# Copying a second block of each cross-partition exchange with GpSimd: a fused cross-attention layer on one Trainium2 core

## Chip, cores and metric

The kernel runs on one core of a Trainium2 chip, all in float32. The metric is the time of one execution on the device in microseconds (us). A change is compared by the median of several runs.

## What is computed

A transformer layer with cross-attention, for 4 batches of 512 rows and 512 features, 16 heads of 32, and an MLP of width 2048:

```python
x = layer_norm(hidden_states, ln1_w, ln1_b)
q = (x @ q_w + q_b).reshape(B, LQ, H, HD).transpose(0, 2, 1, 3)
k = (encoder_hidden_states @ k_w + k_b).reshape(B, LK, H, HD).transpose(0, 2, 1, 3)
v = (encoder_hidden_states @ v_w + v_b).reshape(B, LK, H, HD).transpose(0, 2, 1, 3)
scores = jnp.einsum('bhqd,bhkd->bhqk', q, k) * scale
scores = jnp.where(mask, scores, mask_value)
attn = jax.nn.softmax(scores, axis=-1)
out = jnp.einsum('bhqk,bhkd->bhqd', attn, v)
out = out.transpose(0, 2, 1, 3).reshape(B, LQ, D)
hidden = out @ cproj_w + cproj_b + hidden_states
y = layer_norm(hidden, ln2_w, ln2_b)
y = jax.nn.gelu(y @ fc_w + fc_b, approximate=True)
return hidden + y @ proj_w + proj_b
```

## The kernel before

**Units of attention.** The attention is cut into 16 units w: four batches by four groups of four heads (a group fills the 128 partitions with 4 x 32 features). In the text, 5:1 is unit 5, second half of its 512 query rows. For each quarter of the query rows, `scores` (L510) multiplies q and k on TensorE into four score banks, one a head. `exps` masks a bank and takes its extreme on VectorE (L518), then ScalarE takes exponentials and their sums (L521).

**The exchange.** The probabilities lie with queries on partitions, and the product with v needs keys there. TensorE isn't used for that transposition. VectorE transposes blocks of 32 x 32, each within its group of 32 partitions (`turn`, L529, L536, and L539 for the reciprocal sums) into a buffer tb with four column blocks j. Then block j of partition group i must come to group j, as column block i of a second buffer pT: 16 blocks of 32 partitions x 1088 values for each half of a unit. The four with i = j stay in their group and GpSimd copies them (`stay`, L546). Of the twelve that cross between groups, eleven are transfers from SBUF to SBUF in SyncE's queue (`exchange`, issued by `load`, L327) and one, from group 0 to group 1, is a fifth GpSimd copy (L549). `attend` (L572) multiplies all of pT by v, so it needs all sixteen blocks; L578 scales the product by the reciprocal sums. tb, pT, the 16 units and their two halves make 32 exchanges. tb and pT are both in the tile `swap`.

**Around it.** GpSimd's queue also has bias sums (L330), the weight sums of the MLP's first matrix product (`w_sums`, tile `wsum`, L330 and L333; both products of the MLP are computed with sums of blocks that save multiplications), the layer norm's small power (`ln_rs`, L349 to L357), the sums that apply the first layer norm to a transposed x in batches 1 to 3 (`apply_stats`, L410 and L333), and transfers that it issues itself: stores of the MLP's hidden values (`gelu`, L673, from one of three staging buffers st), of the attention's result (L449) and loads of the mask (L454). ScalarE applies the layer norm's weights after `apply_stats` (`apply_weights`, L421) and copies products into staging buffers (`joins`, L650). `cproj` (L443) is the output projection, `ln_norm` (L362) and `ln_turn` (L369) are the second layer norm and its transposition by TensorE, `fc` and `project` (L625) the MLP.

**The order.** A table of tokens, ORDER, sets the order of all work: each token calls the generator of a piece of work, and each call runs it to its next `yield`. `d:w:half` is `stay`, `e:w:half` is `exchange`, `a` is `attend`, `u` is `scores`. Each engine runs its instructions in the order in which the tokens recorded them. In each exchange `stay` has three steps (two copies, two copies, the fifth), so three `d` tokens, of which other work may stand in between.

Of the kernel before, what the change touches and what calls it, by code (L numbers as in the profile page):

```python
# [86 lines left out]
u:4:2 r:4:0 r:4:1 a:3:0 x:4:2 x:4:2 k:7 r:4:1 a:3:0 x:4:2 r:4:1 r:4:1 x:4:2 c:0:1 d:3:1 v:4 d:3:1 d:3:1
# [21 lines left out]
u:7:3 na:2 g:0:1 j:0:4 wa:2 wa:2 g:0:4 r:7:1 j:0:4 q:8 q:8 g:0:4 d:6:1 d:6:1 d:7:0 d:7:0 d:7:0 e:6:1 lf:0:6 lf:0:6  # L109
  fs:0:6 g:0:4 f:0:3 lh:1 lh:1 e:7:0 e:7:0 e:7:0 x:7:3 x:7:3 r:7:2 x:7:3 x:7:3 a:6:1  # L110
# [4 lines left out]
u:8:3 d:7:1 d:7:1 v:8 j:0:3 f:0:3 f:0:5 k:11 x:8:3 x:8:3 r:8:2 r:8:2 j:0:3 e:8:0 wq:11 lf:1:0 e:8:0 le:3 le:3 lh:1  # L115
  e:8:0 a:7:1 j:0:3 r:8:3 x:8:3 x:8:3 g:0:3 r:8:3 r:8:3
u:9:0 d:8:0 fs:0:5 fs:0:5 cb:1 d:8:0 d:8:0 fs:0:5 g:0:2 v:10 g:0:2 c:1:1 x:9:0 x:9:0 x:9:0 a:7:1 x:9:0 j:0:5 k:11
  c:1:0 r:8:3 c:1:0
u:9:1 x:9:1 x:9:1 r:9:0 f:0:5 f:0:5 j:0:5 fs:0:5 d:8:1 fs:0:6 fs:0:6 d:8:1 d:8:1 cb:1 s2:1 wk:13 e:8:1 wv:12 lx:3
  e:8:1 lx:3 lf:0:7 lf:1:0 wq:12 e:8:1 wv:13 lf:1:1 f:0:7 f:0:5 c:1:3 j:0:5 r:9:1 x:9:1 x:9:1 j:0:5 f:0:5  # L120
u:9:2 g:0:3 j:0:5 r:9:1 r:9:0 r:9:1 s2:1 c:1:3 g:0:5 x:9:2 x:9:2 a:8:0 q:11 x:9:2 a:8:0 r:9:1 x:9:2
u:9:3 r:9:2 j:0:5 x:9:3 q:11 x:9:3 c:1:2 a:8:1 e:9:0 d:9:0 fs:0:7 v:9 c:1:3 fs:0:7 g:0:3 fs:0:7 d:9:0 d:9:0 v:11
# [4 lines left out]
  x:10:1 j:0:7 a:9:0 r2:1 c:1:2 c:1:0 fs:1:0 fs:1:1 fs:1:1 fs:1:1 d:9:1 d:9:1 d:9:1 fs:1:0 fs:1:0 fs:1:0 x:10:1 x:10:1  # L127
# [3 lines left out]
u:10:3 t2:1:3 t2:1:1 t2:1:0 s1:3 t2:1:2 r:10:2 t2:1:2 x:10:3 x:10:3 x:10:3 t2:1:0 v:13 r1:3 d:10:0 d:10:0 d:10:0 g:0:7  # L131
  t2:1:1 a:9:1 ts:3 ts:3 r:10:3 x:10:3
# [14 lines left out]
u:12:3 f:1:4 fs:1:4 fs:1:4 d:11:1 d:11:1 fs:1:3 g:1:2 f:1:4 j:1:3 lf:1:6 wq:15 e:11:1 r:12:1 x:12:3 j:1:4 x:12:3  # L147
  r:12:2 r:12:1 f:1:3 f:1:4 j:1:4 j:1:3 x:12:3 x:12:3
u:13:0 lh:2 fs:1:6 d:12:0 d:12:0 d:12:0 c:2:1 r:12:2 r:12:3 x:13:0 x:13:0 j:1:4 x:13:0 x:13:0 r:12:3 f:1:4 j:1:4
u:13:1 r:12:3 j:1:4 a:11:1 r:12:3 x:13:1 e:12:0 e:12:0 lf:1:7 lp:0 e:12:0 a:12:0 c:2:1 r:13:0 j:1:3 x:13:1 x:13:1  # L150
  x:13:1 a:11:1 d:12:1 d:12:1 d:12:1 fs:1:6 cb:2 fs:1:5 fs:1:5 c:2:0 a:12:0 r:13:0
# [3 lines left out]
  x:13:3 r:13:2 x:13:3 s2:2 c:2:3 fs:1:6 g:1:4 r2:2 d:13:0 d:13:0 d:13:0 a:12:1 a:12:1  # L155
# [84 lines left out]
def xattn_block(ctx: ExitStack, tc: tile.TileContext, x, x_t, encT, mask, q_w, k_w, v_w, c_w, w_fc, p_w, vecs, rows, out):  # L240
    nc = tc.nc
# [48 lines left out]
    pt = ptt.rearrange("p (s c n) -> p s c n", s=3, c=NP)  # L290
# [35 lines left out]
    def load(o, i):  # L326
        nc.sync.dma_start(out=o, in_=i)  # L327
# [215 lines left out]
    def stay(w, half):  # L543
        tb, pT = tb_of[half], pT_of[half]
        for i in range(NI):
            nc.gpsimd.tensor_copy(pT[ts(i, HD), i], tb[ts(i, HD), i])  # L546
            if i % 2:
                yield
        nc.gpsimd.tensor_copy(pT[ts(1, HD), 0], tb[ts(0, HD), 1])  # L549
# [303 lines left out]
    for _ in range(WARM):  # L853
# [70 lines left out]
```

## Time and profile before

| | |
|---|---|
| median of 3 runs | 759.24 us (757.78 to 760.06) |
| the profiled execution | 760.55 us |
| its span, first to last instruction | 758.7 us |
| busy: TensorE (PE) | 750.4 us |
| busy: VectorE (DVE) | 597.8 us |
| busy: ScalarE (ACT) | 403.1 us |
| busy: GpSimd (POOL) | 406.3 us in 433 instructions |

The profile was taken of one execution. A group's row has line, engine, operation, output <- input, count, then busy time in us and mean duration in ns, then the idle time of its engine just before, with what ended it. A row of a timeline has start and duration in us, the same names, and in brackets the engine's idle time before it. Rows of waits read "who <- for whom: us in total, times, longest". SPq is the queue of SyncE, which issues transfers. The profile's line numbers are those of the kernel before.

### The profile page before, as it was taken

What the parts mean: (1) busy time and instruction counts of PE and PEld (TensorE: products, weight loads), DVE (VectorE), ACT (ScalarE), POOL (GpSimd) and SP (SyncE); (2) the same over time, 40 slices, a digit from 0 to 9 for tenths busy, and PEclk for the clock granted to TensorE, in tenths of its full rate; (3) what the DMA queues carried; (4) which work ended last, traced back from release to release, by engine and by line L of the source; (5) the groups of instructions that cost most, each with busy time, mean ns of one, the idle gap of its engine ahead of it and who ended that gap; (6) DMA issues with size and microseconds to landing.
All of it is one profiled execution on the core that took longest, in us unless ns stands there. A gap on an engine that the chain in (4) does not pass through costs nothing.

```text
span 758.7 us, 14111 instructions
## 1 busy us (share of the span) xinstructions
PE 750.4 (99%) x4925; PEld 532.9 (70%) x4925; DVE 597.8 (79%) x1209; ACT 403.1 (53%) x951; POOL 406.3 (54%) x433
## 2 busy tenths in 40 slices
PE   9999999999999999999999999999999999999998
PEld 6464555367665456665655677766888999999997
DVE  3798999999868888876788986644789799786982
ACT  2566766466777776778867686761343221211110
POOL 1166975864996767666858767954401022140232
PEclk9999999999999999999999999999999999999999
DMA  7688877867886797775877598779545647888575
GB/s 267 211 237 231 231 194 225 224 178 215 201 227 201 217 245 241 192 227 141 230 223 202 181 273 240 222 254 317 162 139 175 245 138 160 229 168 261 100 181 111
DMA packets 70598, 157.73 MB, mean 208 GB/s; under 512 B 11448, under 2 KB 24144, under 8 KB 68864
## 3 DMA queue, kind: packets, MB, share of 16 engines
q1 hardware_dynamic: 55328, 126.98, 57.7%
q0 software_dynamic: 15056, 29.84, 15.7%
q8 instruction: 39, 0.64, 0.3%
q14 instruction: 31, 0.25, 0.1%
q10 hardware_dynamic: 144, 0.02, 0.0%
HBM read 73.95 MB, written 25.18 MB: 131 GB/s over the span
## 4 chain that ended last, share of the span: by engine, by line
PE 90%; DMA 4%; SPq 2%; DVE 2%; POOL 1%; issue 1%; ACT 0%; POOLq 0%; ACTq 0%
PE acc L625 34%; PE sc L625 11%; PE sc L510 8%; PE acc L487 8%; PE acc L443 7%; PE acc L497 7%; PE acc L572 7%; PE acc L475 7%; SPq L327 2%; DMA gd<-st 2%; PE acc L369 1%; DMA swap<-swap 1%; DMA ptt<-v_w_dram 1%; DMA pbt<-fc_w_dram 1%; PE acc L854 0%
## 5 line engine op out<-in xcount | busy, mean ns | idle before, releaser
L521 ACT ACTIVATE ptt<-ptt,mn 128x512 f32<-128x512 f32 x256 | 182.9, 716 | 77.8 <-DVE mn L518 77.3
L518 DVE CUSTOM_DVE_ANT_0 ptt<-sc,mix 128x512 f32<-128x512 f32 x256 | 164.5, 679 | 29.4 <-PE sc L510 28.0
L546 POOL COPY swap<-swap 32x1088 f32<-32x1088 f32 x128 | 139.6, 1090 | 56.8 <-DVE swap L539 36.0
L529 DVE STREAM_TRANSPOSE swap<-ptt 128x1024 f32<-128x1024 f32 x64 | 78.8, 1231 | 9.3 <-DMA pbt<-fc_w_dram 4.3
L536 DVE STREAM_TRANSPOSE swap<-ptt 128x1024 f32<-128x1024 f32 x64 | 78.2, 1224 | 1.8 <-ACT ptt L521 1.8
L510 PE MATMUL sc<-pbt 32*128 32x512 f32 x512 | 73.9, 640 | 0.8 <-ACT pbt L489 0.8
L673 POOL DMA_DIRECT2D gd<-st x32 | 24.6, 772 | 91.5 <-ACT st L671 82.7
L650 ACT COPY st<-acc 128x256 f32<-128x256 f32 x96 | 34.3, 367 | 70.8 <-PE acc L625 66.2
L497 PEld LDWEIGHTS acc<-ptt,ext 128*128 128x128 f32 x512 | 58.6, 192 | 9.3 <-issue 2.9
L625 PE MATMUL acc<-ys,wsum 128*128 128x256 f32 x256 | 64.3, 383 | 0.7 <-ACT st L650 0.7
L572 PE MATMUL acc<-swap,mix 128*32 128x256 f32 x1024 | 61.5, 382 | 0.1
L497 PE MATMUL acc<-ptt,ext 128*128 128x128 f32 x512 | 60.9, 277 | 0.3 <-DMA ptt<-v_w_dram 0.3
L625 PE MATMUL acc<-yT,pbt 128*128 128x256 f32 x240 | 59.0, 386 | 1.4 <-DVE mix L578 1.4
L650 ACT COPY xn<-acc 128x128 f32<-128x128 f32 x75 | 18.9, 270 | 77.4 <-PE acc L625 72.6
L475 PE MATMUL acc<-ext,ptt 128*128 128x512 f32 x128 | 58.5, 599 | 0.0
L487 PE MATMUL acc<-ext,ptt 128*128 128x512 f32 x128 | 58.4, 600 | 0.0
L625 PEld LDWEIGHTS acc<-yT,pbt 128*128 128x128 f32 x240 | 44.0, 190 | 20.2 <-issue 6.9
L443 PE MATMUL acc<-mix 128*128 128x512 f32 x128 | 58.0, 599 | 0.0
L625 PEld LDWEIGHTS acc<-ys,wsum 128*128 128x128 f32 x256 | 47.5, 190 | 13.3 <-issue 2.2
L572 PEld LDWEIGHTS acc<-swap,mix 128*32 128x32 f32 x1024 | 30.4, 109 | 31.4 <-issue 9.0
L330 DVE TENSOR_TENSOR st<-acc,st 128x512 f32<-128x512 f32 (+1 forms) x48 | 26.1, 544 | 32.6 <-ACT st L650 22.7
L810 POOL DMA_DIRECT2D swap<-xn x18 | 22.3, 1506 | 52.2 <-DVE xn L330 16.7
(144 smaller groups left out, 1458.2 us busy)
## 6 DMA issues: line engine op xcount, KB each, us to landing
swap<-swap SPq DMA_DIRECT2D x352, 136.0 KB, 3.3
gd<-st POOLq DMA_DIRECT2D x32, 512.0 KB, 4.5
swap<-gd SPq DMA_DIRECT2D x12, 1024.0 KB, 5.1
pbt<-fc_w_dram SPq DMA_DIRECT2D x40, 256.0 KB, 3.9
xn<-x_dram SPq DMA_DIRECT2D x32, 256.0 KB, 4.8
ext<-fc_w_dram SPq DMA_DIRECT2D x24, 256.0 KB, 2.8
swap<-xn POOLq DMA_DIRECT2D x18, 256.0 KB, 4.9
ptt<-k_w_dram SPq DMA_DIRECT2D x16, 256.0 KB, 4.2
```

Of the source, the lines that this page charges most:

```text
L443: nc.tensor.matmul(acc, oT[:, g, ts(t, P)], wc[:, g, :], start=(g == 0), stop=(g == NG - 1))
L475: nc.tensor.matmul(acc, S["wk", w][:, d, :], eT[:, d, :], start=(d == 0), stop=(d == ND - 1))
L487: nc.tensor.matmul(acc, S["wq", w][:, d, :], xT[:, d, :], start=(d == 0), stop=(d == ND - 1))
L497: nc.tensor.matmul(acc[:, ts(t, P)], eT[:, d, ts(t, P)], S["wv", w][:, d, :], start=(d == 0), stop=(d == ND - 1),)
L510: nc.tensor.matmul(sc[h], S["qT", w][r, ts(qt, P)], S["kT", w][r, :], start=True, stop=True)
L518: nc.vector.tensor_tensor_reduce(out=s, in0=sc[h], in1=mb, scale=1.0, scalar=FMAX, op0=ALU.add, op1=ALU.min, accum_out=mn)
L521: nc.scalar.activation(s, s, AF.Exp, bias=mn, scale=-1.0, accum_out=S["sums", w][:, qt, h : h + 1])
L529: nc.vector.transpose(*two_heads[0])
L536: nc.vector.transpose(*two_heads[1])
L546: nc.gpsimd.tensor_copy(pT[ts(i, HD), i], tb[ts(i, HD), i])
L572: nc.tensor.matmul(av[ts(h, HD), : 2 * P].rearrange(shape, **kw), v[:, t, ts(h, HD)], p[t][h], start=(t == 0), stop=(t == NT - 1),)
L625: nc.tensor.matmul(o, x[:, k], y[:, k], start=(k == 0 and not more), stop=(k == n - 1), skip_group_check=more)
```

## The change

The block from group 2 to group 3 (i = 2, j = 3) is copied by GpSimd as well, as a sixth copy in a fourth step of `stay`; `exchange` leaves it out, so it issues ten transfers. It was the first transfer of each exchange.

```diff
@@ -548,13 +550,15 @@
         nc.gpsimd.tensor_copy(pT[ts(1, HD), 0], tb[ts(0, HD), 1])
         yield
+        nc.gpsimd.tensor_copy(pT[ts(3, HD), 2], tb[ts(2, HD), 3])
+        yield
 
     def exchange(w, half):
         tb, pT = tb_of[half], pT_of[half]
         for d in range(1, NI):
             for i in (0, 2, 1, 3):
                 j = (i + d) % NI
-                if (i, j) == (0, 1):
+                if (i, j) in ((0, 1), (2, 3)):
                     continue
                 load(pT[ts(j, HD), i], tb[ts(i, HD), j])
             yield
```

In ORDER each exchange gets a fourth `d` token, straight behind the third; the other tokens and their sequence are as they were. One line of it:

```diff
-u:1:2 r:1:1 q:2 s1:1 x:1:2 x:1:2 x:1:2 x:1:2 k:3 d:0:1 d:0:1 d:0:1 v:0 fs:0:0 r:1:2 r:1:1 q:3
+u:1:2 r:1:1 q:2 s1:1 x:1:2 x:1:2 x:1:2 x:1:2 k:3 d:0:1 d:0:1 d:0:1 d:0:1 v:0 fs:0:0 r:1:2 r:1:1 q:3
```

On TensorE, VectorE and ScalarE the instructions and their order stay the same. The changed file has four more lines, so line 546 is 548 there, 549 is 551, and the added copy is 553.

GpSimd's queue around the copies of 4:0 and 4:1 and the second layer norm's rs of batch 0, before (xn_86 and the like are rows of x, ve_0 and rs_0 the layer norm's numbers):

```order
L330 TENSOR_TENSOR xn_86<-xn_86,row 128x512
L546 COPY swap<-swap 32x1088 x2
L549 COPY swap<-swap 32x1088
L330 TENSOR_TENSOR wsum<-pbt 128x256
L333 TENSOR_TENSOR wsum<-pbt,wsum 128x256
L454 DMA m_73<-mask_dram 128x512
L330 TENSOR_TENSOR mix<-mix,row 128x512
L449 DMA xa_91<-xn_84 128x512
L546 COPY swap<-swap 32x1088 x4
L549 COPY swap<-swap 32x1088
L349 TENSOR_SCALAR ve_0_1324<-mv_0_1187 128x4
L357 TENSOR_TENSOR rs_0_1326<-ve_0_1324,nhalf 128x4
```

and with the change:

```order
L548 COPY swap<-swap 32x1088 x2
L551 COPY swap<-swap 32x1088
L553 COPY swap<-swap 32x1088
L332 TENSOR_TENSOR wsum<-pbt 128x256
L335 TENSOR_TENSOR wsum<-pbt,wsum 128x256
L456 DMA m_73<-mask_dram 128x512
L332 TENSOR_TENSOR mix<-mix,row 128x512
L451 DMA xa_91<-xn_84 128x512
L548 COPY swap<-swap 32x1088 x4
L551 COPY swap<-swap 32x1088
L553 COPY swap<-swap 32x1088
L351 TENSOR_SCALAR ve_0_1324<-mv_0_1187 128x4
```

Two copies more now stand ahead of ve_0 and rs_0.

GpSimd's queue from the copies of 6:0 to the store of the MLP's first hidden values (gd <- st), before:

```order
L546 COPY swap<-swap 32x1088 x2
L549 COPY swap<-swap 32x1088
L330 TENSOR_TENSOR wsum<-pbt 128x256
L333 TENSOR_TENSOR pbt<-pbt 128x256
L333 TENSOR_TENSOR wsum<-wsum,pbt 128x256
L410 TENSOR_TENSOR ext<-ext,xn_84 128x512
L333 TENSOR_TENSOR ext<-ext,xn_82 128x512
L673 DMA gd_95<-st_88 512x1x256
```

and with the change:

```order
L548 COPY swap<-swap 32x1088 x2
L551 COPY swap<-swap 32x1088
L553 COPY swap<-swap 32x1088
L332 TENSOR_TENSOR wsum<-pbt 128x256
L335 TENSOR_TENSOR pbt<-pbt 128x256
L335 TENSOR_TENSOR wsum<-wsum,pbt 128x256
L412 TENSOR_TENSOR ext<-ext,xn_84 128x512
L335 TENSOR_TENSOR ext<-ext,xn_82 128x512
L677 DMA gd_95<-st_88 512x1x256
```

The store stands behind one copy more.

SyncE's queue around the exchange of 1:0, whose transfers are split by the load of the layer norm's numbers (xn_86 <- sd), before:

```order
L327 DMA ext<-x_t_dram 128x512 x2
L327 DMA ext<-encT_dram 128x512 x3
L327 DMA swap<-swap 32x1088 x7
L327 DMA xn_86<-sd_100 128x512
L327 DMA swap<-swap 32x1088 x4
```

and with the change:

```order
L329 DMA ext<-x_t_dram 128x512 x2
L329 DMA ext<-encT_dram 128x512 x3
L329 DMA swap<-swap 32x1088 x6
L329 DMA xn_86<-sd_100 128x512
L329 DMA swap<-swap 32x1088 x4
```

What follows the first transfer of an exchange moves forward by one place.

More of the change, by code (lines that the diff above doesn't have):

```diff
@@ L114 @@
 u:8:2 q:9 r:8:0 r:8:1 r:8:1 x:8:2 j:0:3 r:8:1 q:9 x:8:2 q:10 x:8:2 x:8:2
[L115 to L120, printed above, removed]
+u:8:3 d:7:1 d:7:1 d:7:1 v:8 j:0:3 f:0:3 f:0:5 k:11 x:8:3 x:8:3 r:8:2 r:8:2 j:0:3 e:8:0 wq:11 lf:1:0 e:8:0 le:3 le:3
+  lh:1 e:8:0 a:7:1 j:0:3 r:8:3 x:8:3 x:8:3 g:0:3 r:8:3 r:8:3
+u:9:0 d:8:0 fs:0:5 fs:0:5 cb:1 d:8:0 d:8:0 d:8:0 fs:0:5 g:0:2 v:10 g:0:2 c:1:1 x:9:0 x:9:0 x:9:0 a:7:1 x:9:0 j:0:5
+  k:11 c:1:0 r:8:3 c:1:0
+u:9:1 x:9:1 x:9:1 r:9:0 f:0:5 f:0:5 j:0:5 fs:0:5 d:8:1 fs:0:6 fs:0:6 d:8:1 d:8:1 d:8:1 cb:1 s2:1 wk:13 e:8:1 wv:12
+  lx:3 e:8:1 lx:3 lf:0:7 lf:1:0 wq:12 e:8:1 wv:13 lf:1:1 f:0:7 f:0:5 c:1:3 j:0:5 r:9:1 x:9:1 x:9:1 j:0:5 f:0:5
 u:9:2 g:0:3 j:0:5 r:9:1 r:9:0 r:9:1 s2:1 c:1:3 g:0:5 x:9:2 x:9:2 a:8:0 q:11 x:9:2 a:8:0 r:9:1 x:9:2
-u:9:3 r:9:2 j:0:5 x:9:3 q:11 x:9:3 c:1:2 a:8:1 e:9:0 d:9:0 fs:0:7 v:9 c:1:3 fs:0:7 g:0:3 fs:0:7 d:9:0 d:9:0 v:11
+u:9:3 r:9:2 j:0:5 x:9:3 q:11 x:9:3 c:1:2 a:8:1 e:9:0 d:9:0 fs:0:7 v:9 c:1:3 fs:0:7 g:0:3 fs:0:7 d:9:0 d:9:0 d:9:0 v:11
   fs:0:6 fs:0:7 j:0:7 x:9:3 g:0:5 x:9:3 c:1:2 r:9:2 a:8:1
@@ L146 @@
   x:12:2 r:12:1 q:14 j:1:4
[L147 to L149 removed]
+u:12:3 f:1:4 fs:1:4 fs:1:4 d:11:1 d:11:1 d:11:1 fs:1:3 g:1:2 f:1:4 j:1:3 lf:1:6 wq:15 e:11:1 r:12:1 x:12:3 j:1:4
+  x:12:3 r:12:2 r:12:1 f:1:3 f:1:4 j:1:4 j:1:3 x:12:3 x:12:3
+u:13:0 lh:2 fs:1:6 d:12:0 d:12:0 d:12:0 d:12:0 c:2:1 r:12:2 r:12:3 x:13:0 x:13:0 j:1:4 x:13:0 x:13:0 r:12:3 f:1:4
+  j:1:4
 u:13:1 r:12:3 j:1:4 a:11:1 r:12:3 x:13:1 e:12:0 e:12:0 lf:1:7 lp:0 e:12:0 a:12:0 c:2:1 r:13:0 j:1:3 x:13:1 x:13:1
[L151 removed]
+  x:13:1 a:11:1 d:12:1 d:12:1 d:12:1 d:12:1 fs:1:6 cb:2 fs:1:5 fs:1:5 c:2:0 a:12:0 r:13:0
 u:13:2 r:13:1 x:13:2 g:1:3 f:1:6 c:2:3 r:13:1 g:1:3 c:2:0 x:13:2 x:13:2 g:1:4 g:1:4 r:13:1 x:13:2 c:2:2 lf:2:0 lf:2:0
@@ new lines @@
+  fs:2:4 v:15 g:2:3 x:15:2 a:14:0 f:2:4 j:2:4 f:2:4 f:2:4 j:2:4 d:14:1 d:14:1 d:14:1 d:15:0 e:15:0 e:15:0 e:15:0 f:2:5
+  j:2:2 x:15:2 f:2:4 x:15:2 j:2:4 j:2:5 x:15:2
+u:15:3 f:2:5 d:15:0 d:15:0 d:15:0 f:2:5 x:15:3 x:15:3 r:15:2 j:2:4 f:2:4 j:2:4 j:2:4 a:14:1 a:14:1 r:15:3 g:2:2 g:2:4
+  j:2:5 g:2:4 a:15:0 f:2:5 j:2:5 x:15:3 g:2:2 a:15:0 c:3:0 c:3:0 x:15:3 r:15:2 c:3:1 fs:2:6 fs:2:6 g:2:4 f:2:7 j:2:7
+  r:15:3 s2:3 j:2:5 c:3:1 r:15:3 lf:2:7 fs:2:6 f:2:5 j:2:5 j:2:5 r:15:3 g:2:2 fs:2:7 fs:2:7 fs:2:7 cb:3 la:0:1 lp:4
+  lp:3 lf:3:0 lp:3 lp:5 lf:3:1 lp:7 fs:2:6 d:15:1 c:3:1 fs:2:7 c:3:0 f:2:7 f:2:7 f:2:6 j:2:7 f:2:6 f:2:7 j:2:6 g:2:5
+  j:2:7 f:2:6 j:2:6 lf:3:1 e:15:1 e:15:1 e:15:1 lf:3:0 j:2:7 f:2:7 j:2:7 f:2:6 P:0:1 d:15:1 d:15:1 d:15:1 fs:3:1
+  fs:3:1 fs:3:0 fs:3:0 fs:3:0 fs:3:1 j:2:6 ps:2 j:2:6 ps:4 f:2:6 j:2:6 j:2:6 ps:0 a:15:1 s2:3 la:0:4 lp:7 lh:3 j:2:7
+  cb:3 ps:2 a:15:1 c:3:2 c:3:2 c:3:3 s2:3 c:3:3 s2:3 ps:0 r2:3 fs:3:0 c:3:2 la:0:2 lp:6 P:0:1 hd:0 hd:0 la:0:7 P:0:2
+  pj:0:1 g:2:6 g:2:7 g:2:7 g:2:6 g:2:5 P:0:2 pj:0:2 c:3:3 n2:3 n2:3 g:2:6 g:2:7 fs:3:1 J:0:1 g:2:5 n2:3 n2:3 t2:3:2
+  t2:3:0 t2:3:1 t2:3:0 t2:3:3 t2:3:3 t2:3:2 t2:3:1 y:3 y:3 y:3 ps:2 f:3:0 f:3:1 f:3:1 j:3:1 j:3:0 f:3:1 j:3:1 f:3:0
+  f:3:1 j:3:1 f:3:0 gs:0:5 y:3 gs:0:6 ps:4 gs:0:5 j:3:1 pt:5 pt:6 f:3:1 j:3:0 f:3:0 lf:3:3 f:3:3 j:3:0 j:3:3 j:3:1
+  g:3:1 ps:6 j:3:1 j:3:0 ps:0 pt:3 f:3:0 lr lf:3:3 lf:3:2 fs:3:3 fs:3:3 f:3:3 j:3:0 g:3:1 g:3:0 lf:3:2 fs:3:3 f:3:3
+  j:3:3 ps:2 pt:7 j:3:0 fs:3:3 gs:0:7 fs:3:2 fs:3:2 fs:3:2 fs:3:2 ps:0 f:3:2 g:3:1 f:3:3 f:3:2 j:3:2 j:3:3 g:3:0 f:3:2
+  j:3:2 j:3:3 f:3:3 f:3:2 j:3:3 g:3:3 j:3:2 lf:3:5 g:3:0 ps:6 pt:6 pt:6 xs:0:4 lf:3:4 lf:3:5 j:3:3 j:3:2 ps:4 f:3:5
+  f:3:2 lf:3:4 j:3:2 j:3:2 fs:3:5 pt:5 fs:3:5 gs:0:6 fs:3:5 xs:0:4 ps:4 fs:3:4 fs:3:4 fs:3:5 fs:3:4 fs:3:4 xs:0:4 ps:6
```

77 lines of the change are left out of this document (31 added, 46 removed).

## The prediction

> **What bounds the kernel now.** I read the busy shares first, then what TensorE waits for, and then, place by place, the timelines of the engines that feed it.
>
> ```profile
> PE 750.4 (99%) x4925; PEld 532.9 (70%) x4925; DVE 597.8 (79%) x1209; ACT 403.1 (53%) x951; POOL 406.3 (54%) x433
> ```
>
> TensorE works for 750.4 of 758.7 us, so its idle time is 8.3 us in all. Its waits show how much of that an edit could win:
>
> ```profile
> PE acc L625 <- DVE mix L578: 1.4, 2, 1.0
> PE acc L854 <- POOL nhalf L843: 1.3, 1, 1.3
> PE sc L510 <- ACT pbt L489: 0.8, 1, 0.8
> PE acc L625 <- ACT st L650: 0.7, 2, 0.5
> PE acc L497 <- DMA ptt<-v_w_dram: 0.3, 1, 0.3
> PE acc L625 <- DVE ext L333: 0.2, 1, 0.2
> ```
>
> The columns are total, count and longest, in us. Their sum is 4.7 us, of which 1.3 is the start (the wait for nhalf). So at most 3.4 us are to be gained. There is no such ceiling on a loss: whatever makes TensorE late stays in the time, since it has no idle time to make it up in. So the question is not how busy GpSimd is on average (54%), but where a late GpSimd instruction has TensorE right behind it.
>
> **The prices.**
>
> ```profile
> L546 POOL COPY swap<-swap 32x1088 f32<-32x1088 f32 x128 | 139.6, 1090 | 56.8 <-DVE swap L539 36.0 <-DVE mix L578 10.2 <-PE sc L510 5.7
> L549 POOL COPY swap<-swap 32x1088 f32<-32x1088 f32 x32 | 35.1, 1097 | 1.3
> L327 SPq DMA_DIRECT2D swap<-swap x352: 507/589/2461, 33.2 to 515.7; - x176
> ```
>
> The second row is the copy that already crosses partition groups: 1.097 us, as long as one that stays in its group (1.090). The added copy has the same shape, so I take 1.09 us, and 1.13 us with the 0.04 between two copies (four take 4.47 below). There are 32: 36 us more on GpSimd, all between 33 and 516 us. Removed are 32 of 352 transfers, each a place of 0.59 us in SyncE's queue.
>
> ```profile
> DMA packets 70598, 157.73 MB, mean 208 GB/s; under 512 B 11448, under 2 KB 24144, under 8 KB 68864
> ...
> swap<-swap SPq DMA_DIRECT2D x352, 136.0 KB, 3.3
> ```
>
> A removed transfer gains little: no row of TensorE's waits names an exchange. The relief reaches the path only through other transfers, which get 32 x 136 KB = 4.4 MB of 157.7 MB (2.8%) less company. The waits on st (0.7, partly behind a store) and on v_w (0.3) are all it could shorten: between 0 and 1.0 us. I take 0.3, near the low end, since 2.8% of the 8.1 us which the longest of those stores takes (205.12 to 213.3, below) is 0.2.
>
> An added copy costs nothing where GpSimd next stands idle, and the idle stretch hides it. So I look for stretches in which GpSimd runs on without idle time up to something that TensorE takes at once. A bracket in a row is the idle time just before it.
>
> **Place A, 72 to 96 us.**
>
> ```profile
> 72.89 4.47 POOL L546 COPY swap<-swap 32x1088 f32<-32x1088 f32 x4 [1.39 <-DVE swap L539]
> ...
> 88.91 4.47 POOL L546 COPY swap<-swap 32x1088 f32<-32x1088 f32 x4
> 93.42 1.09 POOL L549 COPY swap<-swap 32x1088 f32<-32x1088 f32 x1
> ```
> ```profile
> 96.18 1.93 PE L572 MATMUL acc<-swap,mix 128*32 128x256 f32 x32
> ```
>
> No row left out has a bracket. Two exchanges lie in one stretch (1:1 and 2:0, with the eight sums of apply_stats between), so two added copies come before 2:0's block is whole: 2 x 1.13 = 2.26 us. TensorE's attention product starts 96.18 - 94.51 = 1.67 us after the last copy. Late by 2.26 - 1.67 = **0.6 us**.
>
> **Place B, 135 to 161 us.**
>
> ```profile
> 135.80 0.63 POOL L449 DMA_DIRECT2D xa<-xn  x1 [3.61 <-DVE xn L330]
> ...
> 142.63 1.08 POOL L549 COPY swap<-swap 32x1088 f32<-32x1088 f32 x1
> ...
> 152.06 1.09 POOL L549 COPY swap<-swap 32x1088 f32<-32x1088 f32 x1
> ...
> 153.51 1.04 POOL L357 TENSOR_TENSOR rs<-ve,nhalf 128x4 f32<-128x4 f32 x1
> ```
> ```profile
> 154.59 0.55 DVE L362 TENSOR_SCALAR xn<-xn,mv,rs 128x512 f32<-128x512 f32 x1 [0.73 <-POOL rs L357]
> ...
> 159.66 0.53 DVE L362 TENSOR_SCALAR xn<-xn,mv,rs 128x512 f32<-128x512 f32 x1
> ```
> ```profile
> 160.09 1.09 PE L369 MATMUL acc<-ident,xn 128*128 128x128 f32 x8
> ```
>
> Again two copies (4:0 and 4:1) and no idle time after 135.80. The small rs of the second layer norm, behind them, comes 2.26 us later. VectorE already waits 0.73 us for it, so all of VectorE's queue behind that L362 moves by 2.26: the score passes that free TensorE's score banks, and the last normalised block, ready at 160.19. TensorE's transpose of that block is the fourth of the eight at 160.09, near 160.5. It can now start at 160.19 + 2.26 = 162.45: **2.0 us** late.
>
> **Place C, 191 to 214 us.**
>
> ```profile
> 191.83 0.58 POOL L400 DMA_DIRECT2D sd<-xn  x1 [0.99 <-ACT xn L397]
> ...
> 199.20 1.09 POOL L549 COPY swap<-swap 32x1088 f32<-32x1088 f32 x1
> ...
> 205.12 0.76 POOL L673 DMA_DIRECT2D gd<-st  x1
> ```
> ```profile
> 213.33 0.37 ACT L650 COPY st<-acc 128x256 f32<-128x256 f32 x1 [1.20 <-DMA gd<-st]
> ```
> ```profile
> 213.85 1.10 PE L625 MATMUL acc<-ys,wsum 128*128 128x256 f32 x4 [0.21 <-ACT st L650]
> ```
>
> Exchange 5:1's copy falls into the 0.99 of idle time. Exchange 6:0's does not: the store of g at 205.12 is issued 1.13 us later. ScalarE waits 1.20 us for it to land, since it needs the staging buffer, and TensorE waits for ScalarE. Every link is already a wait, so it passes in full: **1.1 us**.
>
> **Place D, 346 to 368 us.**
>
> ```profile
> 346.00 1.29 POOL L410 TENSOR_TENSOR ext<-ext,xn 128x512 f32<-128x512 f32 x1 [0.46 <-DMA ext<-x_t_dram]
> ...
> 357.54 2.27 POOL L546 COPY swap<-swap 32x1088 f32<-32x1088 f32 x2 [2.20 <-DVE swap L539]
> ...
> 366.57 0.72 POOL L333 TENSOR_TENSOR wsum<-wsum,pbt 128x256 f32<-128x256 f32 x1
> ```
> ```profile
> 367.96 1.13 PE L625 MATMUL acc<-ys,wsum 128*128 128x256 f32 x4
> ```
>
> From 357.54 GpSimd does not idle; 11:0's added copy lies just before the weight sum at 366.57, which ends at 367.29, 0.67 us before TensorE multiplies by it. Its own copy costs 1.13 - 0.67 = 0.5 us. The copies of 10:0 and 10:1 lie ahead of the apply_stats sums; they bring 2.26 less the 0.46 of idle time = 1.8 us, and the chain goes on through ScalarE (which weights those sums) to the VectorE transposes that GpSimd waits for at 357.54. Between none and all of it arrives, so D costs 0.5 to 2.3. I take **1.5**: the 2.20 us at 357.54 is a wait for this chain's end, as at B, so more of it should pass than not.
>
> **Place E, 474 to 495 us.**
>
> ```profile
> 487.11 4.48 POOL L546 COPY swap<-swap 32x1088 f32<-32x1088 f32 x4
> 491.63 1.08 POOL L549 COPY swap<-swap 32x1088 f32<-32x1088 f32 x1
> ```
> ```profile
> 492.75 3.66 PE L572 MATMUL acc<-swap,mix 128*32 128x256 f32 x64
> ```
>
> The copies of 14:1 end where those of 15:0 begin, so the lag is 2.26. The second half of the 64 matmuls is 15:0's product, near 494.5, 1.8 after 492.71: **0.5 us**.
>
> **The sum.** 0.6 + 2.0 + 1.1 + 1.5 + 0.5 = 5.7, less 0.3 of relief: 5.4 us. After each place GpSimd idles and waits again for engines that follow TensorE, so the lags add up rather than overlap. The profiled execution took 760.55 us (1.85 around the span of 758.7) and would take 766.0. The median of the runs is 759.24, 1.3 lower; on it I forecast **764.6 us**. The bounds of D and the relief give 762.9 to 765.7. A slack misread by 0.5 us at some places widens this to 762 to 767.
>
> **Rivals.**
> *More places.* Lags like those at B may stop TensorE where before it just didn't wait, in the 180s and 208 to 240 us, where GpSimd is at its fullest. Three more places of one copy each are 3.4 us: 768.0. For and against it:
>
> ```profile
> 200.00:220.00 20.00, 18.78 (x144) 13.31 (x136) 13.18 (x31) 13.45 (x34) 18.77 (x19) 1.00 0.90 243
> ```
> ```profile
>   PEld acc L572: 0.3, 1
> ```
>
> In the 20 us from 200 GpSimd is busy for 18.77 (fifth pair), so it hardly absorbs anything there. But of the instructions that wait for the last copy of an exchange, TensorE's attention product is the one in this list, once, for 0.3 us: elsewhere there is slack.
>
> *A clash with VectorE.*
>
> ```profile
> L333 DVE TENSOR_TENSOR ys<-yT,ys x6: 648/692/1395, 172.5 to 454.5; 128x512 f32<-128x512 f32 x6
> L529 DVE STREAM_TRANSPOSE swap<-ptt x64: 1197/1239/1245, 25.5 to 495.2; 128x1024 f32<-128x1024 f32 x64
> ```
>
> A sum whose two inputs both lie in SBUF takes 692 ns at the median and once 1395; the transposes, with one input, stay within 4% though GpSimd works beside many of them. If each of six such sums met a new copy, 6 x 0.7 = 4.2 us of VectorE were lost; the copies fill 36 of 483 us, so one hit, 0.7 us, is likelier: 765.3. [...]
>
> *The other side: not slower.* The mechanism is slack at A, B and E. Each holds two copies in one stretch; if GpSimd gains idle time between them, because the earlier exchange's inputs come earlier with SyncE's queue 0.59 us ahead per exchange, only one copy stands before TensorE, and 1.13 is below the 1.67 and 1.8 of slack at A and E. It decides from a lag under 1.6 us. Then A and E vanish, B halves and C and D stay partly or are paid by transfers that land sooner. With all stalls gone and the full 1.0 of relief it is 758.2; with C and half of B left, 760.3. For it: the exchanges are 48 of the 157.7 MB moved. Against: in both stretches GpSimd's queue is held by its own work, not by a wait that could end sooner.
>
> **How the numbers follow.** Forecast (762 to 767): 0.60. More places (767 to 772): 0.15. The clash by more than one hit (766 to 769): 0.03. The other side (756.5 to 761.5): 0.22. The range of 8 in 10 leaves out the ends of the first and the last rival, about a tenth on each side: 759.0 to 769.5. A measurement of this kernel can tell 0.3% (2.3 us) from no change, so same means 757.0 to 761.5. The other side puts 0.17 into same and 0.05 into faster, though two thirds of the 3.4 us to gain would have to come; the rest, 0.78, is slower.
>
> **What would show it.** GpSimd's busy time should be 441 to 443 us with 192 copies; VectorE's wait on rs at B should grow from 0.73 to about 3; TensorE's own idle time should grow by 4 to 7 us, at A on the exchange, at B on VectorE, at C on the staging copy and at D on wsum. If TensorE's idle time stays near 8.3 us, the slack was larger than I read, and the forecast is wrong. If it grows at other places, the sum was right only by chance.

## The result, and the profile after

The change makes the kernel slower: 768.69 us (767.2 to 769.26, 4 runs) against 759.65 us (757.78 to 760.25, 4 runs) measured beside it, ratio 1.012, 95% interval [1.0097, 1.0144]. That is 9.1 us (7.4 to 10.9). The forecast was 5.4, so the direction held, the time lies inside the range, and the size is too small by 3.7 us. The time lies above the 762 to 767 us that the forecast drew for its own mechanism, in the band that it gave to "more places".

In all that follows, a difference in us is the excess of a ratio times the median of the kernel before in the same comparison. Line numbers are those of each kernel's own file.

The profiled execution after took 767.2 us, with a span of 765.4. The page's engine row and its DMA total answer to those of before:

```profile
PE 753.7 (98%) x4925; PEld 534.1 (70%) x4925; DVE 600.3 (78%) x1209; ACT 403.9 (53%) x951; POOL 442.7 (58%) x465
...
DMA packets 69062, 153.27 MB, mean 200 GB/s; under 512 B 10936, under 2 KB 23632, under 8 KB 67328
...
PE 74%; POOL 13%; DVE 5%; DMA 4%; ACT 2%; issue 2%; SPq 1%; DVEq 0%; POOLq 0%; ACTq 0%
```

GpSimd works 36.4 us more and 4.46 MB less are moved, as computed. The last row is the chain of work that ended last. Here is the same row before:

```profile
PE 90%; DMA 4%; SPq 2%; DVE 2%; POOL 1%; issue 1%; ACT 0%; POOLq 0%; ACTq 0%
```

GpSimd's share of that chain went from 1% to 13%: an engine that is 58% busy has become part of what sets the end. The prices were right: the added copy takes 1106 ns, the one inside its group 1093.

```profile
L548 POOL COPY swap<-swap 32x1088 f32<-32x1088 f32 x128 | 139.9, 1093 | 47.4 <-DVE swap L541 31.4 <-DVE mix L582 9.1 <-PE acc L489 2.2
L553 POOL COPY swap<-swap 32x1088 f32<-32x1088 f32 x32 | 35.4, 1106 | 1.4
```

TensorE's waits after:

```profile
PE acc L629 <- ACT st L654: 2.1, 3, 1.2
PE acc L576 <- POOL swap L553: 1.4, 2, 1.0
PE acc L858 <- POOL nhalf L847: 1.4, 1, 1.4
PE acc L629 <- DVE mix L582: 1.0, 1, 1.0
PE acc L629 <- POOL wsum L335: 0.9, 1, 0.9
PE sc L512 <- ACT pbt L491: 0.8, 1, 0.8
PE acc L629 <- POOL pbt L335: 0.5, 1, 0.5
```

Four of these seven are new or longer, and each names a place: the added copy itself (A, E), the weight sums (D), the staging copy (C and a new place). Place B isn't in the list, though it is the largest, and the span is 6.7 us longer while TensorE's idle time grew from 8.3 to 11.7, by only 3.4. The rest hides in "busy". At B stand eight score matmuls, a pair for each of the four score banks. Below is their row in the timeline, and behind it their row in the view of one line (shortest, median and longest in ns, then the first and the last start in us). Before:

```profile
159.02 1.14 PE L510 MATMUL sc<-pbt 32*128 32x512 f32 x8
```
```profile
L510 PE MATMUL sc<-pbt x8: 587/640/692, 159.0 to 159.6; 32*128 32x512 f32 x8
```

and after, with the wait of the weight loads for VectorE's passes over the banks:

```profile
159.62 3.42 PE L512 MATMUL sc<-pbt 32*128 32x512 f32 x8
162.97 1.09 PE L371 MATMUL acc<-ident,xn 128*128 128x128 f32 x8
```
```profile
L512 PE MATMUL sc<-pbt x8: 587/640/692, 159.6 to 162.5; 32*128 32x512 f32 x8
```
```profile
PEld sc L512 <- DVE mn L520: 1.4, 3, 0.8
```

Each matmul takes as long as before, but before the four pairs run side by side, and now each pair starts when its bank comes free, at 159.62, 160.70, 161.31 and 161.92. So the eight take 3.42 us instead of 1.14, and TensorE is never idle in them: 2.3 of the 3.3 us by which its busy time grew is this delay, called a stall below. That is why I compared the start of the same matmul in both traces, not idle times. The list shows where TensorE fell behind (or caught up), in us:

| place | forecast | after | what it shows |
|---|---|---|---|
| A, 96 us | 0.6 | 1.05 | waits 0.98 for the added copy |
| B, 159 to 161 | 2.0 | 2.29 | score banks, then the transposes |
| C, 214, and 236 | 1.1 | 0.48 + 0.46 | staging copy; at 236 also the score banks |
| D, 362 to 371 | 1.5 | 2.03 | wsum, and pbt one sum earlier |
| F, 473 | - | 1.46 | a store and its staging copy, as at C |
| E, 494.5 | 0.5 | 0.59 | the added copy |
| caught up at 80, 118, 350, 457 | -0.3 | -2.00 | small waits of before that are gone |
| the rest | - | 0.33 | 0.15 of it at the start |
| sum | 5.4 | 6.69 | |

The rows behind A, C, D, F and E, TensorE after:

```profile
97.03 1.93 PE L576 MATMUL acc<-swap,mix 128*32 128x256 f32 x32 [0.98 <-POOL swap L553]
...
217.21 1.10 PE L629 MATMUL acc<-ys,wsum 128*128 128x256 f32 x4 [0.70 <-ACT st L654]
...
366.27 1.13 PE L629 MATMUL acc<-yT,pbt 128*128 128x256 f32 x4 [0.47 <-POOL pbt L335]
...
372.86 1.13 PE L629 MATMUL acc<-ys,wsum 128*128 128x256 f32 x4 [0.95 <-POOL wsum L335]
...
478.69 2.86 PE L629 MATMUL acc<-ys,wsum 128*128 128x256 f32 x12 [1.19 <-ACT st L654]
...
501.14 1.93 PE L576 MATMUL acc<-swap,mix 128*32 128x256 f32 x32 [0.39 <-POOL swap L553]
```

From profile to profile it is 767.2 - 760.55 = 6.65 us. The medians differ by 9.04: 0.90 of the gap is that the profiled execution of before lay that far above its median, and 1.49 that the profiled execution after is the lowest of four. The other three have a mean granted TensorE clock of 0.998 where this one has 1.000. The experiments below show a term in this that the forecast lacked.

### The profile page after: what moved, and what is told of

Its sections match the earlier page's. It is cut to its first block, busy times and chain, and to the rows that moved or that the text cites. A ratio compares the mean times of both kernels' runs of the same rounds, so it can differ in the third digit from the quotient of the medians.

```text
span 765.4 us, 14108 instructions
## 1 busy us (share of the span) xinstructions
PE 753.7 (98%) x4925; PEld 534.1 (70%) x4925; DVE 600.3 (78%) x1209; ACT 403.9 (53%) x951; POOL 442.7 (58%) x465
## 4 chain that ended last, share of the span: by engine, by line
PE 74%; POOL 13%; DVE 5%; DMA 4%; ACT 2%; issue 2%; SPq 1%; DVEq 0%; POOLq 0%; ACTq 0%
PE acc L629 30%; PE sc L629 11%; PE acc L445 7%; PE sc L512 6%; PE acc L489 6%; POOL swap L548 5%; PE acc L576 4%; PE acc L499 4%; PE acc L477 4%; DMA gd<-st 2%; POOL swap L553 1%; POOL swap L551 1%; POOL ext L335 1%; POOL ext L412 1%; DMA swap<-swap 1%
## 5 line engine op out<-in xcount | busy, mean ns | idle before, releaser
L512 PE MATMUL sc<-pbt 32*128 32x512 f32 x512 | 76.3, 640 | 0.8 <-ACT pbt L491 0.8
```

Of the source, the lines that this page charges most:

```text
L512: nc.tensor.matmul(sc[h], S["qT", w][r, ts(qt, P)], S["kT", w][r, :], start=True, stop=True)
```

## The experiments

The theory: only GpSimd's added time costs, only at a few places, and there by "lag less slack": by how much GpSimd comes later, less the time that its result lay ready before TensorE needed it. The rivals: a cost in proportion to the work moved; a clash of GpSimd with other engines' reads; or places other than mine.

### Load without relief, relief without load

Eleven transfers stay, and GpSimd copies the block from group 0 to group 1 twice:

```diff
-        nc.gpsimd.tensor_copy(pT[ts(3, HD), 2], tb[ts(2, HD), 3])
+        nc.gpsimd.tensor_copy(pT[ts(1, HD), 0], tb[ts(0, HD), 1])
-                if (i, j) in ((0, 1), (2, 3)):
+                if (i, j) == (0, 1):
```

> All eleven transfers stay, and GpSimd copies the block from group 0 to group 1 twice: the sixth copy's load on GpSimd's queue alone. Theory 1 (the loss is GpSimd's lag): as slow as the change, +7 to +10 us on the kernel before, perhaps 0.3 more, since no transfer is saved; TensorE late at the same places (after the product of 2:0, near 160, 213, 365 to 372, 478 and 500 us). Rival (the loss comes from leaving out a transfer, which moves SyncE's other transfers forward and so lets them collide): within 2 us of the kernel before.

Measured: 768.34 against 760.19 us, ratio 1.0104 [1.0092, 1.0117], so +7.9 us. The copies alone bring the loss; the transfers play little part in it. The reverse, with no sixth copy and the transfer left out:

```diff
+        if w == 0:
+            nc.gpsimd.memset(pT[ts(3, HD), 2], 0.0)
-        nc.gpsimd.tensor_copy(pT[ts(3, HD), 2], tb[ts(2, HD), 3])
-        yield
```

> The transfer from group 2 to group 3 is left out and no copy takes its place; that block of the buffer is filled with zeros once, in the first unit, so the attention product is computed with a wrong block. The relief alone. Theory 1: 0 to 1.0 us faster than the kernel before, 0.3 forecast, so within noise. Rival (the missing transfer costs): 3 us or more slower.

Measured: 759.28, ratio 0.9989 [0.998, 0.9997], -0.8 us. The relief is real, inside the 0 to 1.0 of the forecast, and larger than the 0.3 I took. TensorE's waits for v_w and st, 0.3 and 0.7 before, are both gone from its list.

### Where: eleven exchanges, and the other twenty-one

The sixth copy is made only in the eleven exchanges that stand before places A to F, ten that the prediction named and 14:0 before F; the others keep their transfer:

```diff
+SIX = ((1, 1), (2, 0), (4, 0), (4, 1), (6, 0), (10, 0), (10, 1), (11, 0), (14, 0), (14, 1), (15, 0))
-        nc.gpsimd.tensor_copy(pT[ts(3, HD), 2], tb[ts(2, HD), 3])
+        if (w, half) in SIX:
+            nc.gpsimd.tensor_copy(pT[ts(3, HD), 2], tb[ts(2, HD), 3])
```

> GpSimd makes the sixth copy in eleven exchanges only: 1:1, 2:0, 4:0, 4:1, 6:0, 10:0, 10:1, 11:0, 14:0, 14:1 and 15:0, those that stand before the places where the trace after shows TensorE late; in the other 21 the transfer stays. Theory 1 (the price is paid at places): +6 to +9 us, nearly all of the change's 9.0. Rival (each copy costs alike): 11/32 of 9.0 = +3.1 us.

Measured: 767.38, ratio 1.0088 [1.0074, 1.0102], +6.7 us. The complement (`not in SIX`):

> The complement: the sixth copy in the other 21 exchanges, the transfer in the eleven. Theory 1: 0 to +1.5 us (only the 0.5 us near 239 us in the trace after is left). Rival (each copy costs alike): 21/32 of 9.0 = +5.9 us.

Measured: 760.11, ratio 1.0004 [0.9995, 1.0014], +0.3 us. TensorE's waits in this kernel, in full:

```profile
PE acc L862 <- POOL nhalf L851: 1.3, 1, 1.3
PE acc L633 <- DVE mix L586: 1.2, 2, 1.0
PE sc L515 <- ACT pbt L494: 0.8, 1, 0.8
PE acc L633 <- DVE ext L338: 0.2, 1, 0.2
```

Nothing that names the exchange's copies, the weight sums or a store is left. One place hides in "busy", as at B: the score group at 234.09 takes 1.93 us, where before it took 1.14.

```profile
234.09 1.93 PE L515 MATMUL sc<-pbt 32*128 32x512 f32 x8
```
```profile
235.05 1.14 PE L510 MATMUL sc<-pbt 32*128 32x512 f32 x8
```

So the twenty-one aren't free everywhere: TensorE loses 0.8 us there and catches up more elsewhere. Even so, two thirds of the added work (21 of 32 copies) cost nothing in sum and one third costs nearly all. A cost in proportion falls.

### How much: half a copy

544 of the 1088 columns are copied and the others transferred, in every exchange:

```diff
-        nc.gpsimd.tensor_copy(pT[ts(3, HD), 2], tb[ts(2, HD), 3])
+        n = PX // 2
+        nc.gpsimd.tensor_copy(pT[ts(3, HD), 2, :n], tb[ts(2, HD), 3, :n])
+                if (i, j) == (2, 3):
+                    load(pT[ts(j, HD), i, n:], tb[ts(i, HD), j, n:])
```

> The sixth copy moves only the first 544 of the 1088 columns (some 0.56 us), a transfer the other 544; eleven transfers stay, one of them half as large. Theory 1 (a lag costs what exceeds the slack of its place): two half lags are 1.2 us, below the slack of 1.67 at A and 1.8 at E, so nothing there; about 1.0 at B, 0.5 at C, 0.4 at D, 0.4 near 478: +2.3 us on the kernel before (1.5 to 3.5). Rival (in proportion to GpSimd's added time): half of 9.0 = +4.5 us.

Measured: 762.03 against 759.52, ratio 1.003 [1.0019, 1.0041], +2.3 us. Half the work costs a quarter of the loss. In its trace A, E and F are gone, and about 1.3 at B, 1.0 at D and 0.2 at C stay. That is lag less slack: the places with slack vanish first. The total came as expected, the parts not quite (1.0, 0.4 and 0.5 there, and 0.4 near 478), so its closeness is partly luck.

### Place B by itself

First the lag of rs is undone alone: the six copies of 4:1 stand behind the small power rs and two stores of the attention's result:

```diff
-  e:4:0 e:4:0 le:2 le:2 c:0:0 v:7 fs:0:0 fs:0:0 cb:0 d:4:0 d:4:0 d:4:0 fs:0:1 x:5:1 c:0:3 fs:0:0 m:1 v:6 c:0:1 d:4:1
-  e:4:1 q:6 wv:8 e:4:1 e:4:1 d:4:1 d:4:1 d:4:1 x:5:1 r:5:0 x:5:1 x:5:1 a:4:0
+  e:4:0 e:4:0 le:2 le:2 c:0:0 v:7 fs:0:0 fs:0:0 cb:0 d:4:0 d:4:0 d:4:0 fs:0:1 x:5:1 c:0:3 fs:0:0 m:1 v:6 c:0:1
+  e:4:1 q:6 wv:8 e:4:1 e:4:1 x:5:1 r:5:0 x:5:1 x:5:1 a:4:0
-u:5:2 v:9 k:8 s2:0 r:5:0 x:5:2 r2:0 r:5:1 n2:0 r:5:1 n2:0 r:5:1 r:5:1 q:6 x:5:2 x:5:2 k:8 x:5:2 c:0:2 c:0:3 n2:0
+u:5:2 v:9 k:8 s2:0 r:5:0 x:5:2 r2:0 r:5:1 n2:0 r:5:1 n2:0 r:5:1 r:5:1 q:6 x:5:2 x:5:2 k:8 x:5:2 c:0:2 c:0:3 d:4:1 d:4:1 d:4:1 d:4:1 n2:0
```

> The changed kernel with one reordering: GpSimd's six copies of 4:1 come after the second layer norm's rs of batch 0 and after the two stores of the attention's result, not before them. Theory 1: VectorE's wait for rs no longer holds the added copy of 4:1, so B (2.3 us in the trace after) is gone and the rest stays: +6.7 us on the kernel before (5.5 to 8). Rival (the price is not paid in GpSimd's order): +8 to +10 us, as the change.

Measured: 765.02, ratio 1.0066 [1.0054, 1.0078], +5.0 us. So 4 us came back, more than the 2.3 of B and than I expected. From profile to profile it is 2.7 (767.2 - 764.52): 1.5 at B, 1.0 at D, and little elsewhere. The rest goes with the clock: all five runs have a mean clock of 1.000. B doesn't vanish, 0.8 of it stays. The copies now run beside VectorE's normalising passes, which take 1.20 and 1.41 us where they took 0.50 and 0.54, and TensorE waits for one:

```profile
155.13 1.20 DVE L364 TENSOR_SCALAR xn<-xn,mv,rs 128x512 f32<-128x512 f32 x1
...
159.55 1.41 DVE L364 TENSOR_SCALAR xn<-xn,mv,rs 128x512 f32<-128x512 f32 x1
```
```profile
153.71 4.71 POOL L548 COPY swap<-swap 32x1088 f32<-32x1088 f32 x4
```
```profile
161.79 0.76 PE L371 MATMUL acc<-ident,xn 128*128 128x128 f32 x5 [0.45 <-DVE xn L364]
```

Then the sixth copy at B alone (`SIX = ((4, 0), (4, 1))`):

> The sixth copy in 4:0 and 4:1 only, the transfer in the other 30 exchanges. Theory 1: B alone, +2.0 to +2.3 us on the kernel before, with TensorE late once, near 160 us. Rival (each copy costs alike): 2/32 of 9.0 = +0.6 us.

Measured: 763.82, ratio 1.0048 [1.0035, 1.0062], +3.6 us. Its runs fall into two groups: two of 762.3 and 762.47 with a mean clock of 1.000, four of 763.72 to 764.68 with 0.997 or 0.998. Its profiled execution is one of the four. The windows below have TensorE's busy time first (instructions in brackets), and after the five engines the granted clock, the third number from the end:

```profile
155.00:162.50 7.50, 7.50 (x24) 3.17 (x23) 5.61 (x15) 3.43 (x8) 3.23 (x6) 1.00 0.19 70
162.50:165.90 3.40, 3.40 (x11) 2.36 (x11) 3.04 (x5) 1.96 (x5) 3.26 (x4) 0.50 0.57 133
165.90:175.00 9.10, 9.10 (x79) 5.70 (x78) 7.69 (x19) 5.84 (x15) 4.57 (x5) 1.00 1.00 268
```

TensorE is busy throughout, yet right behind the stall the clock is halved for 3.4 us, then full again. The eight transposes take 1.85 us instead of 1.09:

```profile
162.36 1.85 PE L374 MATMUL acc<-ident,xn 128*128 128x128 f32 x8
```

The same stretch of the whole change, in its profiled execution, with the same stall, has the full clock:

```profile
163.00:166.40 3.40, 3.40 (x15) 2.05 (x15) 3.38 (x8) 2.04 (x6) 3.26 (x4) 1.00 0.68 177
```

So B costs 2.9 us where the clock holds (762.4 against 759.52) and about 1.7 more where it halves: 3.4 us at half speed lose 1.7. The mean clock of 0.998 in three of four runs of the whole change is worth as much: 0.002 of 765 us is 1.5. Those three weren't profiled. The eleven exchanges alone were, at a mean clock of 0.998, and have the half clock at the same place:

```profile
164.00:167.40 3.40, 3.40 (x11) 2.37 (x12) 3.02 (x6) 2.00 (x5) 3.26 (x4) 0.51 0.63 136
```

### Dose at B

The sixth copy only in 4:1 (`SIX = ((4, 1),)`), so that rs is late by one copy:

> The sixth copy in 4:1 only, ten transfers there; all other exchanges as before. The small power behind it comes one copy, 1.13 us, later instead of 2.26. [...] Rival (a share of the 3.7 us that the two copies cost, in proportion): +1.9 us.

Measured: 761.48 against 760.42, ratio 1.0012 [0.9999, 1.0024], +0.9 us, inside the 0.8 to 1.1 that I forecast by lag less slack (1.13 less about 0.3); the interval reaches from nothing to 1.8, just short of the rival's 1.9. The score group takes 2.27 us, and the granted clock behind it is 1.00. In none of the twelve runs is the mean clock below 0.999:

```profile
160.30 2.27 PE L515 MATMUL sc<-pbt 32*128 32x512 f32 x8
162.50 1.09 PE L374 MATMUL acc<-ident,xn 128*128 128x128 f32 x8
```

Then three copies late (the one of 4:1 made twice):

```diff
         if (w, half) in SIX:
             nc.gpsimd.tensor_copy(pT[ts(3, HD), 2], tb[ts(2, HD), 3])
+            if half:
+                nc.gpsimd.tensor_copy(pT[ts(3, HD), 2], tb[ts(2, HD), 3])
```

> The sixth copy in 4:0 and 4:1, and in 4:1 made twice (the second writes the same values again): GpSimd's small power comes 3.4 us later. [...] Rival 1 (half clock grows with the stall, all in proportion to the 3.7 us of two copies): +5.6 us. Rival 2 (the half clock isn't tied to this stall): +3.1 to +3.4 us.

Measured: 766.05, ratio 1.0073 [1.0054, 1.0093], +5.6 us, what rival 1 had and not my forecast of 4.6 to 4.9: the stall of 3.1 to 3.4 and, as an estimate from the 3.4 us of half clock at B, 1.5 more. The half clock wasn't a fixed price. In the profiled execution it lasted twice as long:

```profile
161.90:168.70 6.80, 6.80 (x17) 3.76 (x16) 5.37 (x13) 4.14 (x11) 5.00 (x6) 0.50 0.51 139
```

Four of the six runs have a mean clock of 0.995 or 0.996, one 0.998. The sixth had 1.000 and took 763.38, +3.0: there the stall alone is seen, near the 3.1 to 3.4 computed. So the runs reach from +3.0 to +6.6 us with their clock, and that the rival's proportion met the median may be chance.

### Filling the gap

B alone again, and 3.6 us of other TensorE work (the k product of unit 9) put where it stalls:

```diff
-u:5:3 a:4:0 n2:0 x:5:3 t2:0:1 t2:0:1 r:5:2 t2:0:0 t2:0:0 x:5:3 r:5:2 x:5:3 k:9 a:4:1 x:5:3 r:5:3 v:9 k:9 y:0
+k:9 u:5:3 a:4:0 n2:0 x:5:3 t2:0:1 t2:0:1 r:5:2 t2:0:0 t2:0:0 x:5:3 r:5:2 x:5:3 a:4:1 x:5:3 r:5:3 v:9 k:9 y:0
```

> The sixth copy in 4:0 and 4:1 only, as in the kernel that lost 3.7 us, and in the order one token moved: the k product of unit 9 (eight matmuls on TensorE, 3.60 us by the group at 161.02) stands ahead of the scores of 5:3 instead of behind the transposes. Theory: the loss is made of TensorE standing still while VectorE's late passes free its score banks (about 2.3 us) and of the half clock that follows (about 1.5 us). With 3.6 us of other work in just that place both go: +0.0 to +0.8 us against the kernel before, and no half clock near 162 us. Rival: the loss comes from the 2.26 us that GpSimd works longer and passes on to everything behind it (VectorE and the later exchanges), not from what TensorE has to do at that moment; then the move changes little and it stays at +3 to +4 us.

Measured: 763.5, ratio 1.004 [1.0023, 1.0056], +3.0 us. Taken alone this speaks for the rival. The control, the same move in the kernel before:

> The control to the kernel before it in this call: the kernel before with the k product of unit 9 moved to the same place and nothing else changed. Both theories: -0.5 to +0.5 us; if it gains or loses more, the move has an effect of its own that must be taken off.

Measured: 764.05, ratio 1.0051 [1.0031, 1.007], +3.9 us. The move itself costs that: VectorE's score passes come 3.6 us later, and TensorE waits for them in the next group of scores, with the half clock behind:

```profile
169.15 1.73 PE L510 MATMUL sc<-pbt 32*128 32x512 f32 x4 [0.45 <-DVE mn L518]
...
170.80:174.20 3.40, 3.40 (x17) 3.40 (x17) 3.17 (x8) 2.42 (x6) 0.00 (x0) 0.51 0.94 224
```

With the move the copies cost nothing further (763.5 against 764.05). Their lag is there, as VectorE waits 3.05 us for rs, but it ends in VectorE's wait for the moved scores: 1.10 us with the copies, 3.38 in the control. That fits lag less slack. It isn't the proof that I wanted, since the gap wasn't filled without a cost, and the move is no mend.

### By place

At the eleven exchanges neither crossing block is copied by GpSimd, at the other twenty-one both are:

```diff
+FOUR = ((1, 1), (2, 0), (4, 0), (4, 1), (6, 0), (10, 0), (10, 1), (11, 0), (14, 0), (14, 1), (15, 0))
-        nc.gpsimd.tensor_copy(pT[ts(1, HD), 0], tb[ts(0, HD), 1])
+        if (w, half) not in FOUR:
+            nc.gpsimd.tensor_copy(pT[ts(1, HD), 0], tb[ts(0, HD), 1])
-                if (i, j) in ((0, 1), (2, 3)):
+                if (i, j) in ((0, 1), (2, 3)) and (w, half) not in FOUR:
```

> A version meant to beat both: in the eleven exchanges of the third run GpSimd copies neither block that crosses (twelve transfers), in the other 21 both (ten transfers). Theory 1: the lag that the kernel before already has at C and near 457 us goes as well, and there are ten transfers fewer in all: 0.5 to 1.5 us faster than the kernel before. Rival (transfers at these places land too late for the attention product, where 2:0, 6:0 and 15:0 have little time): 1 to 3 us slower.

Measured: 760.32, ratio 1.0003 [0.9992, 1.0013]: no difference, less than the 0.5 to 1.5 expected. In its trace TensorE is 1.6 us ahead of the kernel before by 216 us. It loses 0.8 of that in the score group near 234 us, which takes 1.95 us, as it took 1.93 with the sixth copy at the other twenty-one alone.

## Why the prediction was right in direction and short in size

**The bound.** Right: TensorE had no room, and whatever made it late stayed. The eleven exchanges, ten of which I named, bring 6.7 of the 9.1 us, the other twenty-one nothing that can be told from noise (0.3).

**Place A** (0.6, measured 1.05). The slack of 1.67 was read rightly; the lag is 2.47 and not 2.26, as the copy ends at 96.98 instead of 94.51:

```profile
95.89 1.09 POOL L553 COPY swap<-swap 32x1088 f32<-32x1088 f32 x1
```

That makes TensorE 0.85 late at 97.03. The rest is what it had caught up before, at 80 us: a gain ahead of a stall that GpSimd sets only lengthens the stall.

**Place B** (2.0, measured 2.3). Right in mechanism and size. VectorE's wait for rs went from 0.73 to 3.05:

```profile
157.50 0.55 DVE L364 TENSOR_SCALAR xn<-xn,mv,rs 128x512 f32<-128x512 f32 x1 [3.05 <-POOL rs L359]
```

I put the loss on the transposes; most of it sits one step earlier, on the score banks that the same VectorE queue frees. What I did not price is the clock behind it.

**Place C** (1.1, measured 0.5). The store was as late as computed: 209.12 - 205.12 = 4.0, of which 2.9 is TensorE's own lateness. But it landed faster, 7.6 us after its issue instead of 8.2:

```profile
209.12 0.75 POOL L677 DMA_DIRECT2D gd<-st  x1
```
```profile
216.69 0.37 ACT L654 COPY st<-acc 128x256 f32<-128x256 f32 x1 [1.68 <-DMA gd<-st]
```

So the faster landing paid half of the price, as the rival "not slower" had it for this one place. That it comes from the relief isn't shown: in the experiment that keeps all transfers C costs 0.74, only 0.26 more. Of the 0.46 at 236 us, some 0.2 is a wait for a later staging copy, and the rest goes with the score group ahead of it, 1.32 us instead of 1.14. "More places" had that stretch in its list.

**Place D** (1.5, measured 2.0). Inside its bounds of 0.5 to 2.3: most of the chain arrived.

**Place E** (0.5, measured 0.6). Right.

**The step that failed: the search for places, in the sum.** I looked at stores only where ScalarE already waited for one (C). At 14:0 ScalarE waited for TensorE before, so I passed over it. The store comes 1.6 us later than TensorE's own lateness of 4.6 explains, and the wait changes hands. Before:

```profile
467.08 0.71 POOL L673 DMA_DIRECT2D gd<-st  x1
468.13 0.71 POOL L673 DMA_DIRECT2D gd<-st  x1 [0.34 <-issue]
```
```profile
473.78 0.37 ACT L650 COPY st<-acc 128x256 f32<-128x256 f32 x1 [1.35 <-PE acc L625]
```

and after:

```profile
473.25 1.47 POOL L677 DMA_DIRECT2D gd<-st  x2
```
```profile
478.26 0.37 ACT L654 COPY st<-acc 128x256 f32<-128x256 f32 x1 [2.19 <-DMA gd<-st]
```

That is 1.46 us, read from the trace and not tried by itself. It varies with what TensorE caught up at 457 us, just before: 1.46 after a gain of 0.72 here, 1.0 after 0.6 with B's copies moved, 0.4 after 0.4 with the eleven alone, nothing after 0.2 with all transfers kept. So about half of F takes back that gain, as at A, and its net price is 0.7 or less.

**The term that was missing: the clock after a stall**, 1.5 us of the median, estimated from the mean clock of 0.998 in three of its four runs. I priced a stall at its length and gave nothing for the clock. The traces show it at 0.50 for 3.4 us behind the stall with the copies at B alone (162.50 to 165.90) and for 6.8 us behind the stall of three copies (161.90 to 168.70). In the first TensorE wasn't idle in the 7.5 us before the fall, and in the last 3.4 of them it ran the eight score matmuls on 32 rows. The profiled execution of the change has the same stall (3.42 us from 159.62) and a clock of 1.00 behind it. So behind a stall of this length the clock halved in one execution and not in another, and no run shows what decides.

**The relief** (0.3, measured 0.8 alone). Mis-sized. The profile after has 2.0 caught up at four small waits, part of which A and F took back. In the sum F's 1.46 and most of the 2.0 cancel: that the five named places come to 6.4 against 5.7, and the whole profile to 6.7, is in part luck.

**The rivals.** "More places" gave 768.0, near the result, but by three places in the 180s and 208 to 240 us, of which one appeared (0.5). "A clash with VectorE" was read too narrowly. VectorE's busy time grew by 2.5 us, in several small hits and not one of 0.7. The sums that I quoted have the same longest, 1395, but others grew, and so did normalising passes, which have only one large input. In the view of one line's instructions (shortest, median and longest in ns) and in the timeline, before:

```profile
L333 DVE TENSOR_TENSOR ys<-yT x4: 687/692/874, 166.8 to 543.2; 128x512 f32<-128x512 f32 x4
```
```profile
436.02 0.51 DVE L362 TENSOR_SCALAR xn<-xn,mv,rs 128x512 f32<-128x512 f32 x1
```

and after:

```profile
L335 DVE TENSOR_TENSOR ys<-yT x4: 693/880/1132, 169.7 to 549.9; 128x512 f32<-128x512 f32 x4
```
```profile
441.19 0.87 DVE L364 TENSOR_SCALAR xn<-xn,mv,rs 128x512 f32<-128x512 f32 x1
```

No place in the list names them. Where B's copies were moved, such passes did delay TensorE.

"Not slower" falls: the two copies of A, B and E stayed in one stretch each.

**What would show it.** GpSimd's 442.7 us and B's wait came as written. "TensorE's own idle time should grow by 4 to 7 us" was badly put, as it grew by 3.4, because TensorE is busy all through B's stall.

Open is what decides whether the clock halves behind a stall, and the 2 us between the parts and the whole. The eleven and the others give 6.7 + 0.3, the copies and the relief 7.9 - 0.8, both near 7, against 9.1 for the change. The intervals of the eleven (5.6 to 7.8) and of the whole change (7.4 to 10.9, from four runs) touch.

## What to carry to other kernels

Work moved to an engine that is half idle is free or not by place: list the stretches in which that engine runs on without idle time up to something the bottleneck takes at once, and count lag less slack there. Follow every instruction behind the added one, the stores above all, also where their consumer waits for something else today. Compare the starts of the same matmul, since busy time can hide a stall. And price a stall of the matrix engine above its length: here a score group that took 2.3 us longer cost 2.9 us, and 1.7 more where the clock halved.

## What the runs showed of the hardware

- TensorE's granted clock fell to 0.50 for 3.4 us behind a score group of 3.38 us on 32 rows, without idle time, in the profiled execution with the copies at B alone, and for 6.8 us behind the stall of three copies, which had 1.07 us of idle time in it. With one copy at 4:1 (a score group of 2.27 us) it stayed at 1.00.
- In the profiled execution of the whole change the score group took 3.42 us, and the clock behind it was 1.00.
- Eight score matmuls of 32 rows, 640 ns each at the median, took 1.14 us together where they started within 0.6 us, and 3.42 where each pair started as its bank came free. TensorE's busy time counts both in full.
- With B's copies moved, VectorE's normalising pass over 128x512 took 1.20 us beside GpSimd's copies and 1.41 at 159.55. In the profile after it took 0.55 and 0.50 at 157.50 and 158.07, where GpSimd ran no copy.
- GpSimd's added copy of 32x1088 float32, across partition groups, took 1106 ns in the mean, and the copies within one 1093.
